# Issuing a small ScalarE copy, and the apply behind it, at the end of the tile's last quarter

## Chip, cores, metric

One core of one Trainium2 chip. The metric is the device time of one execution in microseconds (us), on that core. The profile is one execution taken by the hardware profiler. Its engines: PE is TensorE's matmuls and PEld its weight loads, DVE is VectorE, ACT is ScalarE, POOL is GpSimd, SP is SyncE. The granted clock is TensorE's clock as the chip allowed it, as a share of full speed (1.00). SBUF and PSUM are the two on-chip memories that hold the kernel's tiles; the matmuls here write to PSUM.

## The reference

Four residual layers over x of 8192 x 8 x 16 x 16 floats, each `x = x + f(groupnorm(x))`. What is at issue lies in layer 0:

```python
def _gn(v, G=4, eps=1e-5):
    g = v.reshape(B_, G, C_ // G, H_, W_)
    m = jnp.mean(g, axis=(2, 3, 4), keepdims=True)
    s = jnp.var(g, axis=(2, 3, 4), keepdims=True)
    return ((g - m) / jnp.sqrt(s + eps)).reshape(v.shape)
# layer 0: a tensor-train operator of three cores
x = x + tt_matvec([core0, core1, core2], _gn(x)) + bias
# layers 1 to 3: 3x3 convolutions with batch norm, quantization, binarized weights (cut)
```

## The kernel before

The kernel is written in a tile framework: the source issues instructions to engines, and a scheduler orders each engine's queue and sets the semaphores. 64 tiles of 128 samples pass through layers 0 and 1 in one loop, four quarters to a tile. Layer 0's norm works on a second layout of the input, xb, two tiles ahead of its use. Here are the parts that matter; `...` marks cuts, and the comments in this and the later cuts are this document's.

```python
def norm_b_stats(t):
    ps = ps_s.tile([P, 3, NB], F32, name=f"stb_{t}", tag="stb")          # PSUM
    nc.tensor.matmul(ps[:, 0:2]..., sum16, sumb..., start=True, stop=True)
    mv = small.tile([P, 2, NB], F32, name=f"mvb_{t}", tag="mvb")          # SBUF, NB = 64
    nc.vector.tensor_copy(mv, ps[:, 0:2])
    ...                                                                   # variance
    nc.gpsimd.tensor_tensor(mv[:, 1], mv[:, 1], mhalf[:, :NB], ALU.pow)   # 1/sigma: the power
    nc.scalar.copy(ps[:, 2], mv[:, 1])                                    # the small copy
    T[t]["stb"] = ps

def norm_b_apply(t):                       # four VectorE instructions: subtract x2, multiply x2
    ps, src = T[t].pop("stb"), T[t].pop("xb")
    xn = wk.tile([P, F], F32, name=f"xn_{t}", tag="xn")
    for k, op, i in ((0, ALU.subtract, src), (2, ALU.mult, xn)):
        for a in range(0, NB, NB // 2):
            cols = slice(a, a + NB // 2)
            nc.vector.tensor_tensor(rows_b(xn)[:, cols], rows_b(i)[:, cols],
                                    ps[:, k, cols].unsqueeze(2).to_broadcast([P, NB // 2, 32]), op)

def expand(t, q, k):                       # half a quarter: 8 expansions, then ScalarE's copy u
    pu = ps_u.tile([P, 4, 2, 2 * R * W], F32, ...)                        # one buffer only
    ...matmul(pu[:, i, j], xv[...], core2[...])...
    nc.scalar.copy(T[t]["u", q][:, 16 * k:16 * k + 16]..., pu...)

for t in range(NT + 2):
    ...
    for q in range(NQ):
        ...
        if q == 3 and t + 2 < NT:
            norm_b_apply(t + 2)
        if t < NT:                         # 8 matmuls po, two expand() of the next quarter in between
            main(t, q, {2: lambda: expand(tn, qn, 0), 6: lambda: expand(tn, qn, 1)} if more else {})
        if q == 1:
            ...
            if t + 2 < NT:
                norm_b_stats(t + 2)
        conv_at(n, conv1)                  # layer 1's conv of an earlier tile: y on ScalarE
```

## Time and profile before

| | before |
|---|---|
| time, median of 3 runs | 5920.27 us (5917.44 to 5920.32) |
| layers 0 and 1 end at | about 3806 us of 5920 |
| one tile there | 58.0 us |
| TensorE idle in it, waiting for u | 6.5 us a tile |

A line of the waits reads: who waited and at which source line, `<-` whom it waited for; then us in total, how often, and the longest. A line of the timeline reads: start, duration, engine, line, operation, tiles; in brackets how long the engine stood idle before it and what ended that. The lines themselves are in the prediction below.

### The profile page before, as it was taken

The page shows a single profiled execution, that of the slowest core. Times are in us where ns is not written, and L with a number is a line of the kernel's source. Part 1 is how long each engine was busy: PE and PEld are TensorE (multiplying, and loading weights), DVE is VectorE, ACT ScalarE, POOL GpSimd, SP SyncE. Part 2 cuts the span into 40 slices and gives each one's busy share as a digit, 9 for nine tenths or more (in the row PEclk, how much of TensorE's full clock was granted, in tenths as well). Part 3 has the DMA queues.
Part 4 walks back from the last instruction along what each step waited for, and adds up shares of the span by engine and source line. Part 5 has one row for each costly group of instructions (what it writes and reads, how often), then busy time and mean ns, then how long its engine had stood idle before and what let it go on. Part 6 is the DMA issues. An engine that isn't in the chain of part 4 may idle for free. (4 is left out here: it accounts for less than half of the span.)

```text
span 5920.5 us, 46345 instructions
## 1 busy us (share of the span) xinstructions
PE 4475.5 (76%) x18501; PEld 2185.7 (37%) x18564; DVE 3305.5 (56%) x3916; ACT 2152.2 (36%) x1473; POOL 2010.5 (34%) x779
## 2 busy tenths in 40 slices
PE   3888989898988889898988889611111688888887
PEld 1444444444444444444444444311111344444444
DVE  4443444444444444444444433499999677777776
ACT  1333333333333333333333333333332443444442
POOL 3223232323223232323232231154444444444443
PEclk9989989898989999898989899855555899999999
DMA  2111111212121111212121111386663122222211
GB/s 80 71 72 71 72 72 71 78 64 78 72 78 72 71 71 71 79 64 79 68 81 72 71 71 43 132 301 247 253 250 136 64 107 100 107 106 106 108 71 57
DMA packets 82952, 583.17 MB, mean 99 GB/s; under 512 B 11568, under 2 KB 11696, under 8 KB 12080
## 3 DMA queue, kind: packets, MB, share of 16 engines
q1 hardware_dynamic: 82736, 580.19, 26.0%
q8 instruction: 148, 2.42, 0.2%
q14 instruction: 68, 0.56, 0.0%
HBM read 324.30 MB, written 255.85 MB: 98 GB/s over the span
## 5 line engine op out<-in xcount | busy, mean ns | idle before, releaser
L308 PE MATMUL po<-u,core 128*128 128x512 f32 x4096 | 2059.2, 635 | 0.6 <-ACT u L299 0.4
L299 ACT COPY u<-pu 128x2048 f32<-128x2048 f32 x512 | 955.0, 1865 | 992.6 <-PE pu L297 992.6
L211 POOL TENSOR_TENSOR mv<-mv,mhalf 128x4 f32<-128x4 f32 x128 | 129.7, 1013 | 3292.9 <-DVE mv L210 3292.9
L308 PEld LDWEIGHTS po<-u,core 128*128 128x128 f32 x4096 | 762.3, 198 | 918.1 <-issue 914.7
L568 PE MATMUL pf<-d,band 128*128 128x480 f32 (+2 forms) x2560 | 873.2, 500 | 198.0 <-DVE d L610 198.0
L297 PE MATMUL pu<-core,xn 32*128 32x256 f32 x8192 | 648.9, 434 | 442.5 <-ACT u L299 421.3
L311 DVE TENSOR_TENSOR x<-po,x 128x512 f32<-128x512 f32 x256 | 177.1, 692 | 1255.5 <-PE po L308 978.2
L297 PEld LDWEIGHTS pu<-core,xn 32*128 32x128 f32 x8192 | 402.7, 201 | 855.0 <-ACT u L299 474.1
L274 POOL TENSOR_TENSOR mvb<-mvb,mhalf 128x64 f32<-128x64 f32 x64 | 675.1, 10548 | 10.6 <-DVE mvb L273 10.6
L568 PEld LDWEIGHTS pf<-d,band 128*128 128x128 f32 x2560 | 450.1, 207 | 590.9 <-issue 579.5
L284 DVE TENSOR_TENSOR xn<-xb,stb 128x1024 f32<-128x1024 f32 x128 | 150.6, 1218 | 593.8 <-PE pu L297 574.2
L223 PE MATMUL gb<-ident,wide_c 128*128 128x128 f32 x128 | 44.0, 447 | 559.6 <-POOL wide_c L216 559.6
L354 ACT ACTIVATE y<-pc,b 128x512 f32<-128x512 f32 x256 | 174.9, 683 | 641.1 <-PE pc L352 641.1
L359 DVE BATCH_NORM_STATS2 bst<-y 128x6 f32<-128x512 f32 x256 | 177.1, 692 | 265.7 <-ACT y L354 265.6
L466 POOL TENSOR_TENSOR x<-x,yl 128x2048 f32<-128x2048 f32 x52 | 234.2, 4503 | 244.2 <-issue 139.9
L247 POOL TENSOR_TENSOR x<-x,bias_t 128x2048 f32<-128x2048 f32 x64 | 288.2, 4504 | 68.5 <-DMA x<-in_xt 68.1
L555 ACT ACTIVATE d<-d,magic 128x2048 f32<-128x2048 f32 x64 | 128.2, 2003 | 429.5 <-DVE d L551 429.5
L350 PE MATMUL pc<-x1n,band 128*128 128x512 f32 x512 | 274.2, 617 | 4.4 <-DVE x1n L339 4.4
L275 ACT COPY stb<-mvb 128x64 f32<-128x64 f32 x64 | 13.8, 216 | 692.0 <-POOL mvb L274 692.0
L351 PE MATMUL pc<-x1n,band 128*128 128x480 f32 x512 | 248.8, 568 | 0.0
L352 PE MATMUL pc<-x1n,band 128*128 128x480 f32 x512 | 247.9, 566 | 0.0
L470 ACT ACTIVATE sq<-x 128x2048 f32<-128x2048 f32 x52 | 99.3, 1910 | 383.5 <-DVE sq_c L209 324.3
(154 smaller groups left out, 5538.1 us busy)
## 6 DMA issues: line engine op xcount, KB each, us to landing
x_d<-x SPq DMA_DIRECT2D x116, 1024.0 KB, 4.8
x<-x_d SPq DMA_DIRECT2D x116, 1024.0 KB, 5.0
xb<-in_xb SPq DMA_DIRECT2D x64, 1024.0 KB, 4.8
x<-in_xt SPq DMA_DIRECT2D x64, 1024.0 KB, 4.9
y_d<-y SPq DMA_DIRECT2D x64, 1024.0 KB, 3.8
yl<-y_d SPq DMA_DIRECT2D x64, 1024.0 KB, 9.0
out_dram<-x SPq DMA_DIRECT2D x52, 1024.0 KB, 3.9
out_dram<-keep SPq DMA_DIRECT2D x12, 1024.0 KB, 3.8
```

What stands on the lines that cost most here:

```text
L247: nc.gpsimd.tensor_tensor(v, v, bias0_t.unsqueeze(1).to_broadcast([P, P, W]), ALU.add)
L274: nc.gpsimd.tensor_tensor(mv[:, 1], mv[:, 1], mhalf[:, :NB], ALU.pow)
L297: nc.tensor.matmul(pu[:, i, j], xv[rows, (2 * q + k) * 2 + j], core2[rows].rearrange("p a n -> p (a n)"), start=True, stop=True)
L299: nc.scalar.copy(T[t]["u", q][:, 16 * k:16 * k + 16].rearrange("p b n -> p (b n)"), pu.rearrange("p i j n -> p (i j n)"))
L308: nc.tensor.matmul(samples(po), core01[:, r], u[:, :, r, :], start=(r == 0), stop=(r == R - 1))
L311: nc.vector.tensor_tensor(x[:, cols], po, x[:, cols], ALU.add)
L350: nc.tensor.matmul(pv, band1[:, 1], xv, start=True, stop=False)
L351: nc.tensor.matmul(pv[:, :, 1:W], band1[:, 0], xv[:, :, 0:W - 1], start=False, stop=False)
L352: nc.tensor.matmul(pv[:, :, 0:W - 1], band1[:, 2], xv[:, :, 1:W], start=False, stop=True)
L359: nc.vector.bn_stats(bst[:, q], y[:, q * BANK:(q + 1) * BANK])
L466: nc.gpsimd.tensor_tensor(x2t, x1t, yt, ALU.add)
L568: nc.tensor.matmul(o, w, i, start=(n == 0), stop=(n == len(taps) - 1))
```

## The change

The intent: ScalarE's queue should not stand still for GpSimd's power in the middle of a tile. So the small copy leaves `norm_b_stats` and is issued, with the apply, after the last quarter's matmuls.

```diff
             nc.gpsimd.tensor_tensor(mv[:, 1], mv[:, 1], mhalf[:, :NB], ALU.pow)
-            nc.scalar.copy(ps[:, 2], mv[:, 1])
-            T[t]["stb"] = ps
+            T[t]["stb"], T[t]["mvb"] = ps, mv
+
+        def norm_b_copy(t):
+
+            nc.scalar.copy(T[t]["stb"][:, 2], T[t].pop("mvb")[:, 1])
 ...
-                if q == 3 and t + 2 < NT:
-                    norm_b_apply(t + 2)
                 if t < NT:
 ...
                     main(t, q, ...)
+                if q == 3 and t + 2 < NT:
+                    norm_b_copy(t + 2)
+                    norm_b_apply(t + 2)
```

(The loop that starts the first two tiles calls the copy directly ahead of the apply.)

More of the change, by code (lines that the diff above doesn't have):

```diff
@@ L377, in tile_net @@
             norm_b_stats(t)
+            norm_b_copy(t)
             norm_b_apply(t)
```

## The prediction

> **What bounds the kernel now.** I read the page's slices first, then busy time by stretch, the groups, the waits of the first stage, and one tile's timeline, engine by engine. The slices show three stages: about 24 of 40 slices (some 3540 us) of layers 0 and 1, a middle stage bound by VectorE, and a last stage. The changed lines run in the first stage alone; the 64 tiles take about 58 us each there (the statistics' matmuls of two successive tiles start at 1503.42 and 1561.45 us).
>
> Busy time by stretch (start:end, length, then busy time of each engine; the last numbers are granted clock, DMA share and GB/s):
>
> ```profile
> 120.00:3540.00 3420.00, 3038.36 (x13255) 1409.00 (x13258) 1450.13 (x1823) 1265.36 (x883) 953.76 (x235) 0.91 0.19 72
> ```
>
> TensorE is busy 3038 of 3420 us, and no other engine half of it. So TensorE bounds the stage, and what can be won is its idle time, or the slow clock after it. The waits of this stage, between 500 and 3400 us (50 tiles; total, times, longest), then the group that is waited for:
>
> ```profile
> ACT stb L275 <- POOL mvb L274: 525.2, 50, 10.5
> ...
> DVE xn L284 <- PE pu L297: 472.3, 50, 9.8
> ...
> PE pu L297 <- ACT u L299: 327.2, 50, 6.5
> ```
>
> ```profile
> L274 POOL TENSOR_TENSOR mvb<-mvb,mhalf 128x64 f32<-128x64 f32 x64 | 675.1, 10548 | 10.6 <-DVE mvb L273 10.6
> ```
>
> TensorE waits once a tile, 6.5 us, for the copy u of ScalarE; ScalarE waits once a tile, 10.5 us, for GpSimd's power of 10.55 us, ahead of the small copy of 1/sigma. One tile in order of time shows that these are one wait (the lines are from the listings of GpSimd, ScalarE and TensorE):
>
> ```profile
> 1507.37 10.55 POOL L274 TENSOR_TENSOR mvb<-mvb,mhalf 128x64 f32<-128x64 f32 x1
> ...
> 1506.76 0.69 ACT L354 ACTIVATE y<-pc,b 128x512 f32<-128x512 f32 x1 [3.16 <-PE pc L352]
> 1517.95 0.22 ACT L275 COPY stb<-mvb 128x64 f32<-128x64 f32 x1 [10.50 <-POOL mvb L274]
> 1518.10 1.86 ACT L299 COPY u<-pu 128x2048 f32<-128x2048 f32 x1
> ...
> 1508.70 1.15 PE L297 MATMUL pu<-core,xn 32*128 32x256 f32 x16
> 1509.77 3.70 PE L308 MATMUL po<-u,core 128*128 128x512 f32 x8
> 1520.02 2.09 PE L297 MATMUL pu<-core,xn 32*128 32x256 f32 x16 [6.54 <-ACT u L299]
> 1522.03 3.78 PE L308 MATMUL po<-u,core 128*128 128x512 f32 x4
> ```
>
> The expansion pu of the quarter is ready at 1509.9 us, but ScalarE's copy of it into u stands behind the small copy, and that stands behind the power. pu has a single buffer, so TensorE's next expansion waits until 1520.02 us. After the gap it also runs slower: 16 expansions take 2.09 us and four matmuls 3.78 us, against 1.15 and 1.98 us later in the same tile.
>
> **What the Trainium skill says.** "PSUM — Partial Sum Buffer", section "Engine vs sequencer instructions", says that the queues of ScalarE, VectorE and GpSimdE are strictly first in, first out. The trace agrees: the copy u was ready at 1509.9 us and ScalarE stood idle, yet it began at 1518.10 us, behind the small copy. "TensorE: Matmul & The Clock Gate", section "Step-by-step: what each phase is for", says that matmuls stay in program order and only weight loads are pulled ahead; the gap of 6.54 us, in which no matmul goes past the one that waits, agrees. What follows from both is that a place in an engine's built queue decides here, not a place in the source. The same page, section "What's actually happening", says that TensorE falls to half clock after an idle window of about 3.4 us; the 16 expansions after 6.54 us of idle took 1.8 times as long, which agrees roughly.
>
> **The change part by part.** As the source reads, it takes ScalarE's copy (216 ns each, 64 times, 13.8 us in all) and the four VectorE instructions of the apply (1.2 us each) out of the places behind the statistics and ahead of the last quarter, and puts them after that quarter's matmuls. It adds and removes no instruction. Its intent is plain: four copies u and one copy y would then stand ahead of the small copy, and the power would finish beside them.
>
> But a scheduler stands between this source and the engines' queues, and the profile of before already shows that it doesn't keep the source's order. In the source the apply follows the whole of the third quarter, its add included; on VectorE two halves of the apply run first, then that add, then the other two halves:
>
> ```profile
> 1522.24 2.35 DVE L284 TENSOR_TENSOR xn<-xb,stb 128x1024 f32<-128x1024 f32 x2 [9.44 <-PE pu L297]
> 1525.85 0.69 DVE L311 TENSOR_TENSOR x<-po,x 128x512 f32<-128x512 f32 x1 [1.26 <-PE po L308]
> 1526.46 2.34 DVE L284 TENSOR_TENSOR xn<-xn,stb 128x1024 f32<-128x1024 f32 x2
> ```
>
> So I built both kernels and compared the instructions of each engine in their built order. The raw comparison differs in nearly every row, but only because the source lines shifted and the running numbers of buffers changed. With those two taken off, and the tile, quarter and half in each name kept, nothing is left:
>
> ```
> engine   rows before   rows after   rows that differ
> PE              5121         5121                  0
> DVE             3147         3147                  0
> ACT             1475         1475                  0
> POOL             786          786                  0
> SP               569          569                  0
> ```
>
> I went one step further and compared the full instruction records, with shapes, offsets, semaphores and the values waited for: 0 differences in any of the five queues, which hold 11405 records of TensorE, 4193 of VectorE, 2006 of ScalarE, 1228 of GpSimd and 1145 of SyncE, waits and register moves included. The addresses of all 4508 allocations are the same too. In the build of the changed kernel ScalarE's order at the fourth tile is: y of tile 0 quarter 3, the copy of 1/sigma of tile 4, the two copies u of tile 2 quarter 3, y of tile 1 quarter 0. That is the order of before, with the copy ahead of the two u that it delays.
>
> My reading of why: the scheduler puts into a queue what is ready in its own estimate of time, and takes the source's order only among several that are ready. If it holds the power for far shorter than 10.55 us, the copy looks ready while ScalarE has nothing else, wherever the source has it. This is inferred from the orders, and no duration of the scheduler's is known to me. The sum doesn't need it.
>
> The sum: instructions removed 0, added 0, moved 0 on every engine; waits changed 0; addresses changed 0. Change of time 0 us, so 5920.27 us, rounded to **5920 us**.
>
> **The rivals.** First, the order takes effect as the source says. Then TensorE loses its wait: 6.5 us a tile, 62 tiles, some 403 us (the whole program has 421.3 us of it). The slow stretch after it goes as well: 2.09 - 1.15, 3.78 - 1.98 and 1.22 - 1.02 us make 2.94 us a tile, 182 us in all. That is 585 us, or a time near 5335 us (10% less), an estimate. The profile speaks for this wait being on the path; the equality of the built queues speaks against its being touched. It would need a difference that I did not compare.
>
> Second, the later apply delays a buffer: xn comes later, the next tile's expansions wait, the source's move costs time. At worst some 5 us of apply a tile come onto TensorE's path, 62 times 4.8 us, 298 us, near 6220 us. The expansion that needs it is a whole tile (58 us) away, which makes it small even were it moved; and nothing is moved.
>
> Third, the machine code is the same but the execution isn't: another chip, another phase of the granted clock, another layout in memory. The three runs of before lie within 2.9 us (0.05%), and executions of one kernel agree mostly within 0.3%, which is 18 us. This sets my range.
>
> **Range and chances.** With an equal program only scatter is left. The range is 5908 to 5932 us, four times the scatter of before on each side. Faster by over 2% would need 118 us, a slow state or a comparison gone wrong: 1% for faster, 1% for slower, 98% within 2%.
>
> **What would show it.** In the profile after: the wait of ScalarE's small copy on the power still 64 times and 692 us in all, TensorE's wait for u still near 421 us, busy times of every engine within a fraction of a per cent, and 46345 instructions. The timeline still has the copy ahead of two u in the third quarter and a gap of 6.5 us on TensorE. I am wrong if the copy stands behind the last quarter's u on ScalarE, or if that gap is gone; then the comparison of the built queues did not describe what ran.

## The result, and the profile after

The changed kernel took 5919.55 us (median of 4, 5916.60 to 5922.32); the kernel before, in the same series, 5920.30 us. The ratio is 0.9999, with a 95% interval of 0.9982 to 1.0016: the same. Ratios here and below are those on record, from fast runs alone; they are not quite the ratios of the medians quoted.

The profile after answers line by line to the one before. The source lines have shifted (275 is now 279, 297 is 300, 299 is 302). Busy time by stretch, with the same columns as in the prediction:

```profile
120.00:3540.00 3420.00, 3038.44 (x13255) 1409.27 (x13257) 1449.71 (x1823) 1264.64 (x883) 953.48 (x235) 0.91 0.19 72
```

The waits between 500 and 3400 us:

```profile
ACT stb L279 <- POOL mvb L274: 524.9, 50, 10.5
...
PE pu L300 <- ACT u L302: 327.1, 50, 6.5
```

ScalarE at the same tile, in order of time:

```profile
1506.74 0.69 ACT L357 ACTIVATE y<-pc,b 128x512 f32<-128x512 f32 x1 [3.16 <-PE pc L355]
1517.92 0.22 ACT L279 COPY stb<-mvb 128x64 f32<-128x64 f32 x1 [10.50 <-POOL mvb L274]
1518.07 1.86 ACT L302 COPY u<-pu 128x2048 f32<-128x2048 f32 x1
```

TensorE is busy 3038.44 us of the stretch, against 3038.36. Both waits are there, as long and as often. The small copy still stands directly ahead of the copy u that it delays, and it begins at 1517.92 us where it began at 1517.95. Moving it in the source moved nothing on the chip. What stayed open was why, and whether the change would have worked if it had reached the queue.

### The profile page after: what moved, and what is told of

Read it like the earlier page. It is cut to its first block, busy times and chain, and to the rows that moved or that the text cites. A ratio compares the mean times of both kernels' runs of the same rounds, so it can differ in the third digit from the quotient of the medians.

```text
span 5917.1 us, 46408 instructions
## 1 busy us (share of the span) xinstructions
PE 4483.4 (76%) x18564; PEld 2186.4 (37%) x18564; DVE 3302.7 (56%) x3916; ACT 2151.5 (36%) x1473; POOL 2009.4 (34%) x779
## 5 line engine op out<-in xcount | busy, mean ns | idle before, releaser
L198 DVE TENSOR_REDUCE ends<-x 128x64 f32<-128x1024 f32 x208 | 238.3, 1204 | 0.0
```

Of the source, the lines that this page charges most:

```text
L198: nc.vector.tensor_reduce(dst[:, a:b], samples(src)[:, a:b], AX.X, op)
```

## The experiments

All kernels ran with three rounds against the kernel before, which took 5917 to 5918 us in these series. Results are right unless said otherwise.

**What the scheduler does with the source's place (builds only, nothing ran).** I built variants and compared each engine's whole queue, instruction records with wait values, against a partner:

```
variant                                               differs from           records that differ
copy and apply at the front of the last quarter       the kernel before                        0
copy and apply in the next tile's third quarter       the kernel before                        0
power twice: source as before / as after              each other                               0
power 40 times, source as after                       the copy still stands ahead of both u
128x2048 addition x2 ahead of the power               the copy still stands ahead of both u
128x2048 addition x4 ahead of the power, before/after each other                               0
   ... the copy now stands between the two u of the third quarter, in both
```

So the place in the source, over a whole tile, changes nothing, and enough added GpSimd work ahead of the power moves the copy by one place whatever the source says. This agrees with the prediction's reading that the queue is filled by readiness in the scheduler's own estimate, and it suggests how far off that estimate is for the power: 40 powers (an estimate of 422 us on the chip, at 10.55 us each) did not move the copy, while of the additions two did not and four did (an estimate of 9 and 18 us, at the 4.5 us that the bias addition of that size takes). On the chip the one power delays both u already. The scheduler's own durations were not measured.

**held_end_q3: the change, held in the queue.** An order edge puts the copy behind the last copy u that the source has before it. `issue_after` fixes the place in the engine's queue; it adds no wait.

```diff
-            nc.scalar.copy(T[t]["stb"][:, 2], T[t].pop("mvb")[:, 1])
 ...
+                with tc.issue_after(last_u[0].ins):   # last_u: the newest copy u
 ...
+                nc.scalar.copy(T[t]["stb"][:, 2], T[t].pop("mvb")[:, 1])
```

> The changed kernel with one constraint more: the copy of 1/sigma may stand on ScalarE only behind the last copy u that the source has before it. In the build it now stands behind the four copies u and the one y that the source puts ahead of it. Theory (ScalarE's queue order at the power is what TensorE pays for, and the change failed only because the scheduler undid it): TensorE's wait for u of 6.5 us a tile and about 2.9 us of slow clock a tile go, 62 tiles, 585 us: near 5335 us. Rival A (the copy is not what holds TensorE, or the wait comes back as another one): within 60 us of 5920. Rival B (the later apply on VectorE delays the next tile's xn): over 5920.

It took 5351.38 us, ratio 0.9043 (0.9028 to 0.9058). Busy time between 500 and 3000 us, then what is left of ScalarE's wait for the power over the whole program:

```profile
500.00:3000.00 2500.00, 2493.70 (x11461) 1151.91 (x11459) 1242.83 (x1593) 1092.56 (x767) 840.08 (x207) 1.00 0.24 86
```

```profile
ACT stb L281 <- POOL mvb L275: 34.5, 2, 17.3
```

TensorE is now busy 2493.7 of 2500 us, and its granted clock is 1.00 instead of 0.91. ScalarE waits for the power twice, at the start, not 64 times. The time is 16 us above the 5335 us expected, and TensorE's wait in the loop is gone: the theory holds and both rivals fall. So the change's intent was right, and only its means had no effect.

**pow2_after: the power doubled, nothing held.**

```diff
+            waste = small.tile([P, NB], F32, name=f"waste0_{t}", tag="waste")
+            nc.gpsimd.tensor_tensor(waste, mv[:, 1], mhalf[:, :NB], ALU.pow)
             nc.gpsimd.tensor_tensor(mv[:, 1], mv[:, 1], mhalf[:, :NB], ALU.pow)
```

> The changed kernel with the power done twice (the first into a tile that nobody reads): GpSimd's 10.55 us become 21.1 us a tile; the built order on ScalarE is again the same with and without the change. Theory (the power is on TensorE's path through the copy): 10.55 us more a tile, 62 tiles, 654 us: near 6574 us, and TensorE's wait near 17 us a tile. Rival (the power is hidden, the wait has another source): 5920 within 60 us.

It took 6578.34 us, ratio 1.1116: 661 us more, where 654 were expected. TensorE's wait:

```profile
PE pu L302 <- ACT u L304: 635.1, 37, 17.2
```

17.2 us in place of 6.5, in each of 37 tiles between 500 and 3000 us. The power lies on TensorE's path with its whole length. That the sum came so near is in part luck: a tile became 10.24 us longer (the statistics' matmuls of successive tiles are 68.27 us apart, against 58.03), because the slow stretch after the gap lost 0.4 us, and 62 times that is 635 us. Another 22.7 us lie at the start, where TensorE waits 31.8 and 25.8 us for the first tiles' norm in place of 21.2 and 13.7; the expectation had left these out.

**held_end_q3_pow2: both.**

> The constraint and the doubled power together. Theory: with the copy behind the last quarter's u, the second power lies beside other work, so the time is that of the constraint alone within 20 us (near 5335). Rival (GpSimd or the buffers bind as well): up to 654 us more than with the constraint alone.

It took 5375.79 us, 24 us more than with the hold alone; I had allowed 20. The loop has hidden the second power. What remains is at the start, where TensorE waits for the first tiles' norm and no earlier tile is there to hide it. TensorE's waits, first with the hold alone, at one instruction:

```profile
78.93 1.21 PE L307 MATMUL pu<-core,xn 32*128 32x256 f32 x2 [21.17 <-DVE xn L294]
...
96.58 2.09 PE L307 MATMUL pu<-core,xn 32*128 32x256 f32 x16 [13.66 <-ACT u L309]
```

With the power doubled as well, the waits of the whole program:

```profile
PE pu L309 <- DVE xn L296: 31.7, 1, 31.7
PE pu L309 <- ACT u L311: 25.8, 1, 25.8
```

21.2 became 31.7 and 13.7 became 25.8: 22.6 of the 24 us.

**held_q3_front: the smallest hold.** Copy and apply stand ahead of the last quarter, as early as the kernel before had the apply, and the copy is held behind the two u of the third quarter's expansions only.

```diff
+                if q == 3 and t + 2 < NT:
+                    norm_b_copy(t + 2)          # held behind the newest u, as above
+                    norm_b_apply(t + 2)
                 if t < NT:
 ...
-                if q == 3 and t + 2 < NT:
-                    norm_b_copy(t + 2)
-                    norm_b_apply(t + 2)
```

> The smallest move that should do: copy and apply stand in the source ahead of the last quarter's matmuls, and the copy may stand on ScalarE only behind the two copies u of the third quarter's expansions. In the build it is behind these two and ahead of y of the next quarter. Theory: the power ends about 8 us after ScalarE got the first of these u, and TensorE has two matmul pairs and the conv's three taps to do by then, so it waits for next to nothing: within 20 us of the 5351 us that the later place gave. Rival (the place must be behind the whole last quarter, as the change had it): TensorE waits 2 us or more a tile for the next u, 124 us or more in all: 5475 us or above.

It took 5332.37 us (5329.25 to 5335.19), ratio 0.9008 (0.8992 to 0.9023), the fastest kernel with a right result. ScalarE and, below it, GpSimd at one tile:

```profile
1528.53 1.86 ACT L309 COPY u<-pu 128x2048 f32<-128x2048 f32 x1 [2.79 <-PE pu L307]
1531.86 0.22 ACT L281 COPY stb<-mvb 128x64 f32<-128x64 f32 x1 [1.47 <-POOL mvb L275]
1532.88 0.69 ACT L364 ACTIVATE y<-pc,b 128x512 f32<-128x512 f32 x1 [0.80 <-PE pc L362]
```

```profile
1521.29 10.55 POOL L275 TENSOR_TENSOR mvb<-mvb,mhalf 128x64 f32<-128x64 f32 x1
```

ScalarE still waits 1.5 us for the power, but nothing is ready for it then: y starts 0.8 us after the copy has ended, as soon as TensorE's conv is done. Two places in the queue were the whole matter. A tile takes 48.5 us (the first copies u of the tile start at 1499.12 and 1547.64), against 58.0 before: 9.5 us times 62 tiles is 590 us, and 586 were measured. Against the later hold, 48.5 stands against 48.9 us a tile; there TensorE is not quite full (2493.7 against 2500.0 of 2500 us). These 6.3 us of idle time are some 0.12 us a tile, so only a part of the 0.4 us; what makes the rest was not tested and stays open.

**no_copy: no small copy at all.** The multiply reads 1/sigma from SBUF, and nothing is held.

```diff
-            nc.scalar.copy(ps[:, 2], mv[:, 1])
-            for k, op, i in ((0, ALU.subtract, src), (2, ALU.mult, xn)):
+            for stat, op, i in ((ps[:, 0], ALU.subtract, src), (mv[:, 1], ALU.mult, xn)):
```

> The kernel before without ScalarE's small copy: the apply on VectorE multiplies by 1/sigma from SBUF. Nothing is moved. Theory (what costs is that ScalarE stands still for the power, not that the power takes long): ScalarE waits no more, TensorE's 6.5 us go; VectorE waits for the power instead, but the add of the quarter stands ahead of that wait: near 5335 us. Rival (the wait moves to VectorE and TensorE then waits for the adds and for xn): 5700 to 5950 us.

It took 5338.74 us, ratio 0.9021. With ScalarE out of it, its standing still is gone, and the same gain comes without any move. VectorE had the room, but it pays something that I had not expected. VectorE, then GpSimd, at one tile:

```profile
1536.88 0.68 DVE L310 TENSOR_TENSOR x<-po,x 128x512 f32<-128x512 f32 x1
1537.95 6.66 DVE L283 TENSOR_TENSOR xn<-xn,mvb 128x1024 f32<-128x1024 f32 x2 [0.38 <-POOL mvb L274]
```

```profile
1537.88 4.52 POOL L247 TENSOR_TENSOR x<-x,bias_t 128x2048 f32<-128x2048 f32 x1
```

Two multiplies take 6.66 us instead of about 2.4, and the bias addition of 4.52 us starts just ahead of them. Under held_q3_front the same addition (1531.80, 4.54 us) lies beside the subtracts, which have one input in PSUM, and they keep their 2.35 us:

```profile
1532.11 2.35 DVE L294 TENSOR_TENSOR xn<-xb,stb 128x1024 f32<-128x1024 f32 x2 [1.00 <-ACT stb L281]
```

The Trainium skill, "SBUF — State Buffer", section "SBUF: two separate sides", says that a VectorE instruction with two SBUF inputs contends with a GpSimd instruction that reads SBUF, and that the one that starts second blocks for the other's whole instruction. The trace agrees: 4.3 us more beside an addition of 4.5 us. The last experiment tests it.

**pow_as_add: the power made cheap.** A wrong result (relative error 0.42): `ALU.pow` became `ALU.add` at line 274. Against the changed kernel only 64 GpSimd records differ, these additions; the copy still stands ahead of both u.

> A wrong result on purpose: the changed kernel with GpSimd's power of 64 columns replaced by an addition of the same shape; order, waits and buffers stay as they are, with the copy ahead of the two u. Theory (the wait is the power's duration at that place in the queue): the addition takes well under 1 us, the small copy is done before u is ready, TensorE doesn't wait: 5335 to 5355 us with nothing moved. Rival (the place in the queue or the semaphore from GpSimd costs in itself): 5600 us or more.

It took 5309.11 us, ratio 0.8972, below the range I had given. The addition takes 318 ns (20.4 us for 64):

```profile
L274 POOL TENSOR_TENSOR mvb<-mvb,mhalf 128x64 f32<-128x64 f32 x64 | 20.4, 318 | 9.9 <-DVE mvb L273 9.9
```

The place in the queue costs nothing by itself: only the duration at that place does. My range had left out the start again. TensorE's two waits there fall from 21.1 and 13.7 us under held_q3_front to 11.2 and 3.4, 20 of the 23 us between the two kernels.

**no_copy_pow2: has VectorE room for more?** no_copy with the power doubled as above.

> The apply from SBUF without ScalarE's copy, with the power done twice. It asks whether VectorE has room to take the wait that ScalarE had none for. VectorE is busy 60% of this stage and its apply has until the end of the last quarter. Theory (room is there, but not for 10.55 us more: VectorE stands still from about 3 us after the third quarter's add until the power ends, some 10 us, and the next add and the statistics of the tile come late): TensorE loses a part of 10.55 us a tile; I expect 5345 to 5700 us. Rival (VectorE has no room, all of it shows): 5990 us. Second rival (all of it is hidden): within 10 us of 5339.

It took 5958.11 us, ratio 1.0067: 619 us more than no_copy, outside my range and near the rival of no room. TensorE and VectorE at one tile:

```profile
1552.85 0.97 PE L353 MATMUL pc<-x1n,band 128*128 128x480 f32 x2
1561.83 3.47 PE L309 MATMUL po<-u,core 128*128 128x512 f32 x4 [8.01 <-DVE x L312]
```

```profile
1551.58 6.65 DVE L285 TENSOR_TENSOR xn<-xn,mvb 128x1024 f32<-128x1024 f32 x2 [11.00 <-POOL mvb L276]
1558.16 0.68 DVE L360 BATCH_NORM_STATS2 bst<-y 128x6 f32<-128x512 f32 x1
1558.76 2.32 DVE L263 TENSOR_REDUCE sumb<-xb 128x32 f32<-128x1024 f32 x2
1561.01 0.68 DVE L312 TENSOR_TENSOR x<-po,x 128x512 f32<-128x512 f32 x1
```

VectorE stands 11.0 us at the multiply. Then 6.65 us of multiplies, the statistics and the sums stand ahead of the add that frees po's PSUM buffer, for which TensorE waits 8.0 us. The wait that had left ScalarE came back on VectorE.

**no_copy_pow2_short_add: how much of that is the SBUF port.** The same with the bias addition on 8 instead of 128 samples; its result is wrong.

```diff
-            nc.gpsimd.tensor_tensor(v, v, bias0_t.unsqueeze(1).to_broadcast([P, P, W]), ALU.add)
+            nc.gpsimd.tensor_tensor(v[:, :8], v[:, :8], bias0_t.unsqueeze(1).to_broadcast([P, 8, W]), ALU.add)
```

> A wrong result on purpose: the apply from SBUF with the power done twice, and GpSimd's bias addition, which follows the power, cut to a sixteenth (4.5 us become some 0.4 us). In the run before it the first multiply from SBUF took up to 5.5 us in place of 1.2 when that addition ran beside it, and TensorE waited 8.0 us a tile for VectorE. Theory (VectorE's multiply with both inputs in SBUF stands still while GpSimd reads SBUF): both multiplies take 2.4 us, TensorE's wait falls by 4.3 us a tile to 3.7 us: 5958 - 62 x 4.3 = 5690 us. Rival (the multiply is slow for another reason, its shape or the wait counted in): it stays at 5.5 us and the time at 5958 us.

It took 5700.37 us, ratio 0.9632. The multiplies (min/median/max in ns), then TensorE's wait:

```profile
L285 DVE TENSOR_TENSOR xn<-xn,mvb x128: 1210/1218/1469, 82.1 to 3455.8; 128x1024 f32<-128x1024 f32 x128
```

```profile
PE po L309 <- DVE x L312: 182.2, 46, 4.0
```

The longest multiply fell from 5.53 to 1.47 us, and TensorE's wait from 8.0 to 4.0 us a tile. So of the 619 us, some 258 came from the blocked multiply. The rest, 361 us, is put down to a power too long for VectorE's slack; that is what is left over, and no run isolates it.

| kernel | median us | ratio |
|---|---|---|
| changed kernel | 5919.55 | 0.9999 |
| held_end_q3 | 5351.38 | 0.9043 |
| held_end_q3_pow2 | 5375.79 | 0.9084 |
| held_q3_front | 5332.37 | 0.9008 |
| no_copy | 5338.74 | 0.9021 |
| pow_as_add (wrong result) | 5309.11 | 0.8972 |
| pow2_after | 6578.34 | 1.1116 |
| no_copy_pow2 | 5958.11 | 1.0067 |
| no_copy_pow2_short_add (wrong) | 5700.37 | 0.9632 |

## Why the prediction was right

- **Equal queues, equal time.** Right: 5919.55 us against 5920 predicted, and every group and wait named agrees within 0.2%. The one sign that failed is the count of instructions: I had expected 46345, and the profile after has 46408. The profile before had 18501 matmul records for 18564 weight loads, the one after 18564 for both, so 63 records were missing from the trace before; the programs are the same.
- **What bounds the first stage.** Right, and now tested. The wait scales with the power (6.5 to 17.2 us when it is doubled), vanishes when the copy is held two places further back, and vanishes when the copy or the power's duration is taken away. I misread the length of the stage from the slices: it ends near 3806 us, not 3540. The sum used tiles, so no number hangs on it. The slow stretch after the gap is the clock, as I had it, and the profile shows it directly: in the kernel before the granted clock is 0.50 from 1516 to 1525 us and 1.00 again from 1526 to 1530, and with the hold it is 1.00 from 500 to 3000. "Agrees roughly" was too kind on one point, though: at this tile the clock fell some 2.3 us after TensorE's last matmul had ended (1513.5 us), under pow2_after at one tile some 5.3 us after it, so the 3.4 us that I quoted are no fixed delay here.
- **The scheduler puts in what is ready in its own estimate.** Supported by the builds above: neither place nor repeated powers moved the copy, large additions did. The estimate itself stays unseen.
- **The first rival, the order as written.** It did not come about, but its size was right: 585 us estimated, 566 measured with the later hold (5917.03 to 5351.38) and 586 with the earlier. Its two terms add to 9.48 us a tile, and the tile became 9.5 us shorter.
- **The second rival, a late apply that delays xn.** Wrong also for the held kernel: TensorE has no wait for xn in the loop there. Only 0.4 us a tile separate the late hold from the early one.
- **Scatter, and the third rival.** The runs after lie within 5.7 us, well inside the range, so the equal program also ran equally. I named two scatters, 18 and 2.9 us; the range of 12 us on each side comes from the second.

## What to carry to other kernels

Where a scheduler stands between source and queue, compare the built queues before believing in a move; they were equal here, and so was the time. To move an instruction, give it an order edge, or take away the instruction that blocks. When an in-order engine waits for a long operation, ask what stands behind the waiting instruction and who waits for that: two places in ScalarE's queue were worth 10% here, and the same wait put on VectorE was free with one power, but not with two.

## What the Trainium skill lacked or had wrong

- "GPSIMD Engine Reference" has times for an elementwise addition but none for a power: 128x64 took 10.55 us as a power and 0.32 us as an addition of the same shape, a factor of 33.
- No page has that an instruction's place in the source need not be its place in the engine's queue: three moves, over up to more than a tile's length, gave records with 0 differences here, and an order edge was worth 586 us.
